# Sums of a graph layer turned in blocks on VectorE, attributes moved by five bits, and rows stored in rounds

## The chip, the core and the metric

The kernel runs on one core of one Trainium2 chip. The metric is the device time of one execution in microseconds, the median of the runs shown. The engines are called as in the profile: PE (TensorE), DVE (VectorE), ACT (ScalarE), POOL (GpSimd) and SP (SyncE, which here only issues DMAs).

## The reference

A message passing layer with a residual and a layer norm, over 50,000 nodes of 160 numbers (64 scalars `s`, 32 vectors `v` of 3) and 1,650,000 edges sorted by their destination. 800,000 of the edges are random, 800,000 are the same ones turned round, and 50,000 are loops from a node to itself.

```python
ss, vv = s[src], v[src]
e0, e1 = sh[:, 0:1], sh[:, 1:4]                  # 4 attributes per edge
dot = einsum('eui,ei->eu', vv, e1)
out0 = C0 * (ss * e0 @ W1 + dot * INV3 @ W2)
p3 = (ss @ W3)[:, :, None] * e1[:, None, :] * INV3
p4 = einsum('eui,uw->ewi', vv * e0[:, :, None], W4) * INV3
p5 = einsum('eui,uw->ewi', cross(vv, e1[:, None, :]), W5) * INV6
out1 = C1 * (p3 + p4 + p5)
m_agg = segment_sum(concatenate([out0, out1]), dst)
h = (m_agg scalars @ Ws, m_agg vectors @ Wv), scaled
x = layernorm(x + x + relu(h))
```

A message is linear in the row of the source and linear in the 4 attributes. So the kernel first sums, for each node and each attribute k, attribute k times the row of the source (4 x 160 numbers per node), and applies the weights to the sums: one matrix of 160 x 160 per attribute, in which W1 to W5 are already multiplied by Ws and Wv.

## The kernel before

**The units of work.** A unit is 128 edges. A group is 6 units, whose destinations fit into 32 consecutive nodes (W = 32 slots). Two groups make a pair (12 units), four groups a chunk (128 slots), and 20 groups, or 10 pairs, share one load of edges (table s). There are 1044 pairs, 522 chunks and 391 blocks of 128 output nodes. One long unrolled loop runs over the pairs.

**One pair.** POOL gathers the rows of the sources by 12 indirect DMAs, one per unit, into a tile `xg` (L304); there are four such tiles (`rows`, bufs=4). DVE makes `hot` (which of the 32 slots an edge falls into, L313) and `ha` (`hot` times each of the 4 attributes, L316), with three buffers. PE multiplies (L326): for each unit `ha` (128 edges x 4 x 32) against the gathered rows (128 edges x 160), summed over 6 units into `ps`, which holds 4 x 32 rows (attribute and slot) of 160 for each of two groups and has two buffers. ACT copies `ps` to `A` (L329).

**One chunk.** `turn` brings the feature axis to the partitions: PE transposes the four `A` in two parts, features 0 to 127 and 128 to 159 (`pt`, L564), and ACT copies each part to `at` (L567). `apply_weights` makes 8 products on PE (4 attributes x 2 parts of the features, `phc`, L578) and ACT copies the result to `hp` (L582).

**One block.** The loops from a node to itself are not gathered: `ahead` loads the block's own rows `xt` and their attributes `sa` (L593, L597), `own` transposes `xt` on PE (`ptx`, L616, two parts, with an ACT copy each, L617), multiplies by the weights (`yx`, L622, L623) and sums them with `sa` on DVE (`t`, L627, L629). `nodes` makes `hot2` (L606), which maps the slots of the chunks that may hold nodes of this block to its 128 nodes, and `block` sums the chunks' `hp` by it on PE (`phb`, L639, one product per chunk). How many chunks a block takes follows from bounds on where a chunk's nodes can lie (`off`, `low`, `high`, L200 to L206). Then follow relu, the residual and the norm on DVE (L175 to L190, with a root on ACT, L184), and SP sends `o` out (L737).

**The packs.** The loops must be taken out of the list of edges, and their attributes collected. The first 100 groups take the edges as they are; for the others 17 packs of 120 rows of 790 edges are worked on, beside the pairs, on DVE. A pack is a list of steps, spread over the pairs until it is due (`todo`, L796): read; `count`, `mark`, `examine`, `where` (find the loops and number them); `collect` (L471: for each of 31 places and 4 attributes one multiply with a sum over a stretch of the row, into `mine`); `shift` (L503 to L510: the remaining edges, `prow`, move left by 1, 2, 4, 8 and 16 places as the bits of their distance `far` say); then SP stores the rows to `edges` and `mine` to `selves` in DRAM at places held in registers (L543), first the even rounds of 10 rows, then the odd ones, then the heads of the rows again. Later loads of edges (L240) and `ahead` read these tables.

**What sets the order.** SP's order is the one in which the program is written (a manual schedule for SP, L766). PE, DVE, ACT and POOL run in the order that a scheduler finds; each engine then runs its list strictly in that order. `psM`, two buffers, is shared by `pt`, `phc`, `ptx`, `yx` and `phb`.

In the pair loop the change and the prediction touch these lines:

```python
rows = gather(placed[s], (g - s * SG) * G, ng * G, ...)     # L774
...
has[p + 1] = spread(placed[s1], (g1 - s1 * SG) * G, ng1 * G) # L778
sums.append(group_sums(p, rows, has.pop(p)))                 # L779
...
after_pair(p + 1, do_turn, c, sums)                          # L805
...
after_pair(p + 2, do_weights, c)                             # L811
```

## Time and profile before

| what | before |
|---|---|
| median of 3 runs (lowest, highest) | 20348.03 us (20332.03 to 20362.42) |
| the profiled execution | 20370.95 us |
| its span, first to last instruction | 20369.2 us |
| mean granted clock of PE | 0.663 |
| busy: POOL, PE, DVE, ACT | 11850.9, 10539.8, 6385.3, 1564.6 us |
| matmuls on PE | 47031 |
| gathers on POOL | 12522 |

A row of a group gives line, engine, operation, tiles and shapes, the count, then the busy time with the mean in ns of one, then the idle time of the engine just ahead of them and what ended it. A product in fp32 stands as two matmuls in these counts (25044 for 12522), a transpose as one. A row of waits gives the engine and what it did next, what it waited for, the time in all, how often, and the longest. "issue" is time in which the engine waited for nothing that the profile shows, "remote" is a release by something that it doesn't name. Times of a matmul's end are modelled.

### The profile page before, as it was taken

How to read it: one execution, taken by the hardware profiler on the slowest of the kernel's cores; microseconds unless marked ns; L12 is line 12 of the kernel's file. 1: busy time of each engine (PE TensorE's matmuls, PEld its weight loads, DVE VectorE, ACT ScalarE, POOL GpSimd, SP SyncE). 2: the span in 40 equal slices, each digit the busy share in tenths (PEclk: the TensorE clock that was granted, in tenths of full speed). 3: DMA queues.
4: the chain of work that ended last, by engine and by line, in shares of the span. 5: the costliest groups of instructions: out<-in, count | busy, mean ns of one | idle time of the engine just before them, and what ended most of it. 6: DMA issues, size and time to landing. Idle time of an engine off the chain costs nothing. (4 is left out here: it accounts for less than half of the span.)

```text
span 20369.2 us, 146272 instructions
## 1 busy us (share of the span) xinstructions
PE 10539.8 (52%) x47031; PEld 8362.9 (41%) x47032; DVE 6385.3 (31%) x15106; ACT 1564.6 (8%) x3876; POOL 11850.9 (58%) x12536
## 2 busy tenths in 40 slices
PE   5455545455454545555454545545454554545455
PEld 3343434334343434444443434434343443434444
DVE  3342423323242323323142333324232232413222
ACT  0000000000000000000000000000000000000000
POOL 6455655555565655555565655556565555656565
PEclk6666666666666666666666666666666666666666
DMA  2222222222222222222222222222222222222222
GB/s 63 58 55 62 58 63 58 59 60 61 60 59 63 58 59 61 61 60 57 65 57 64 58 60 61 60 57 61 63 57 59 61 61 58 60 61 59 58 61 55
DMA packets 809692, 1217.63 MB, mean 60 GB/s; under 512 B 283401, under 2 KB 587942, under 8 KB 804932
## 3 DMA queue, kind: packets, MB, share of 16 engines
q0 software_dynamic: 601056, 1026.60, 19.5%
q1 hardware_dynamic: 207256, 181.09, 3.3%
q8 instruction: 374, 6.13, 0.1%
q14 instruction: 398, 3.26, 0.1%
q10 hardware_dynamic: 608, 0.55, 0.0%
HBM read 1135.20 MB, written 72.13 MB: 59 GB/s over the span
## 5 line engine op out<-in xcount | busy, mean ns | idle before, releaser
L304 POOL DMA_INDIRECT xg<-in_x,si x12522 | 11846.6, 946 | 8441.8 <-issue 3609.6
L326 PE MATMUL ps<-xg,ha 128*128 128x160 f32 x25044 | 4929.5, 354 | 1846.3 <-issue 1601.1
L326 PEld LDWEIGHTS ps<-xg,ha 128*128 128x128 f32 x25044 | 4459.7, 233 | 2263.0 <-issue 1972.5
L316 DVE TENSOR_TENSOR ha<-hot,pk 128x1536 f32<-128x1536 f32 x1044 | 1820.5, 1747 | 3301.8 <-remote 2346.1
L616 PE MATMUL ptx<-ident,xt 128*128 128x128 f32 (+2 forms) x782 | 263.5, 337 | 3389.7 <-ACT xT L617 2563.9
L640 DVE TENSOR_TENSOR phb<-phb,t 128x160 f32<-128x160 f32 x391 | 129.8, 332 | 5466.4 <-remote 2231.4
L564 PE MATMUL pt<-ident,A 128*128 128x128 f32 (+1 forms) x4174 | 908.9, 361 | 1577.3 <-ACT hp L582 507.9
L616 PEld LDWEIGHTS ptx<-ident,xt 128*128 128x128 f32 (+2 forms) x782 | 100.4, 128 | 3545.3 <-ACT xT L617 2653.7
L471 DVE SCALAR_TENSOR_TENSOR pra<-marks,prow 120x236 bf16<-120x236 f32 (+40 forms) x2924 | 1491.9, 510 | 26.1 <-DVE pra L471 5.5
L578 PE MATMUL phc<-BWa,at 128*128 128x160 f32 x4176 | 940.7, 371 | 916.5 <-issue 741.4
L639 PE MATMUL phb<-hp,hot 128*128 128x160 f32 x4694 | 1057.9, 386 | 570.0 <-issue 487.4
L564 PEld LDWEIGHTS pt<-ident,A 128*128 128x128 f32 (+1 forms) x4174 | 557.5, 153 | 1901.9 <-issue 678.6
L578 PEld LDWEIGHTS phc<-BWa,at 128*128 128x128 f32 x4176 | 802.1, 243 | 1024.6 <-issue 834.3
L639 PEld LDWEIGHTS phb<-hp,hot 128*128 128x128 f32 x4694 | 951.4, 259 | 638.5 <-issue 533.1
L627 DVE TENSOR_SCALAR t<-yx,sa 128x160 f32<-128x160 f32 x391 | 149.6, 383 | 3274.9 <-PE yx L623 2287.1
L578 PE MATMUL phc<-BWb,at 32*128 32x160 f32 x4176 | 948.3, 374 | 397.3 <-issue 307.0
L623 PE MATMUL yx<-BWb,xT 32*128 32x320 f32 x1564 | 974.7, 718 | 182.4 <-issue 139.7
L578 PEld LDWEIGHTS phc<-BWb,at 32*128 32x128 f32 x4176 | 773.9, 236 | 545.8 <-issue 449.9
L567 ACT COPY at<-pt 128x512 f32<-128x512 f32 (+1 forms) x1044 | 600.5, 580 | 4909.6 <-remote 2561.2
L622 PE MATMUL yx<-BWa,xT 128*128 128x320 f32 x1564 | 923.2, 688 | 5.5 <-issue 3.1
L329 ACT COPY A<-ps 128x320 f32<-128x320 f32 x1044 | 440.0, 422 | 4581.1 <-remote 2777.5
L629 DVE SCALAR_TENSOR_TENSOR t<-yx,sa,t 128x160 f32<-128x160 f32 x1173 | 448.0, 382 | 847.1 <-remote 454.1
(147 smaller groups left out, 4931.8 us busy)
## 6 DMA issues: line engine op xcount, KB each, us to landing
xg<-in_x,si POOLq DMA_INDIRECT x12522
edges<-prow SPq DMA_DIRECT2D x1994, 18.5 KB
r<-edges SPq DMA_DIRECT2D x99, 360.0 KB
selves<-mine SPq DMA_DIRECT2D x1992, 0.5 KB
xt<-in_x SPq DMA_DIRECT2D x390, 80.0 KB
out<-o SPq DMA_DIRECT2D x390, 80.0 KB
pra<-in_attr SPq DMA_DIRECT2D x16, 1481.2 KB
edges<-prow SPq DMA_DIRECT2D x997, 0.8 KB
```

The source lines that it names most:

```text
L304: nc.gpsimd.indirect_dma_start(out=xg[:, j, :], out_offset=None, in_=x, in_offset=bass.IndirectOffsetOnAxis(ap=placed[0][:, u + j:u + j + ...
L316: nc.vector.tensor_tensor(ha[:, :n], hot[:, :n].unsqueeze(2).to_broadcast([P, n, NK, W]), pk[:, :, u:u + n].rearrange("p k u -> p u k").un ...
L326: nc.tensor.matmul(ps[:, j // G, :], ha[:, j].rearrange("p k w -> p (k w)"), xr, start=j % G == 0, stop=j % G == G - 1)
L329: evict(A[:, :ng], ps[:, :ng])
L471: nc.vector.scalar_tensor_tensor(T["waste"][:n, w0:w1], T["marks"][:n, w0 - a:w1 - a], float(w + 1), T["rows"][:n, w0:w1, 2 + k], op0=ALU. ...
L564: nc.tensor.transpose(pt[:f1 - f0, g, :], A[:, i, f0:f1], ident)
L567: evict(at[:, :, :ng].rearrange("f k g w -> f g k w"), pt[:f1 - f0, :ng].rearrange("f g (k w) -> f g k w", w=W))
L578: nc.tensor.matmul(ph[:ng * W], at[:, k, :ng].rearrange("f g w -> f (g w)"), bw[:, k, :], start=i == 0, stop=i == 2 * NK - 1)
L622: nc.tensor.matmul(y[:nb], xT[:, 0, :nb], BWa[:, ks, :], start=True, stop=False)
L623: nc.tensor.matmul(y[:nb], xT[:D - P, 1, :nb], BWb[:, ks, :], start=False, stop=True)
L629: nc.vector.scalar_tensor_tensor(t[:nb], y[:nb, i], sa[:nb, k:k + 1], t[:nb], op0=ALU.mult, op1=ALU.add)
L639: nc.tensor.matmul(ph[:nb], hot2[:r, i, :nb], hp[:r], start=i == 0, stop=i == len(cs) - 1)
```

## The change

**Sums.** `group_sums` no longer copies `ps` to `A`. DVE transposes `ps` in blocks of 32 x 32 straight into `sums`, a tile [128, 5, 4, 32] per chunk: partition k * 32 + f holds feature 32 b + f of attribute k, for block b of the features, group and slot. `turn` is gone with its transposes on PE and its copies on ACT. The weights are laid out to match (`BWk`: the same 128 rows, 5 blocks), and `apply_weights` makes 5 products over 128 rows in place of 8. `BWk` and `BWh` are built through a table in DRAM at the start.

**The block's own rows.** `own` transposes two parts of 80 features, copies both at once on ACT, and multiplies by `BWh`, the weights in two parts of 80; the number of products stays.

**The packs.** 16 packs of 128 rows in place of 17 of 120. `where` and `collect` go. `aim` takes for each loop the distance from its place in the row to its number, as five bits plus a mark of 32 (L468 and on of the new file); the attributes `pra` move left by these bits as the rows do, in a pass of their own ahead of that for `prow`; `pick` clears what has no mark, and one reduction over the row sums the places w, w + 32, w + 64 and so on into `mine`. The rows are stored in 16 successive rounds of 8, and the heads of one round only. Two more empty steps stand ahead of the stores.

**Bounds and checks.** The bounds on a chunk's nodes are set for each tenth of the edges by themselves, so that a block takes 4 or 5 chunks (before 5 or 6): 1737 products `phb` in place of 2347. The checks on these bounds run some 9 pairs ahead of the end and not behind the last pair.

```diff
+    cuts = sorted({0, NH // QG, NCH} | {round(i * NCH / 10) for i in range(10)})
...
+        off = 5 * math.sqrt(n_edges * max(0, t * (1 - t))) / (degree - 1) + 10
+        bounds += [(-off, 0.75 * step + W + off)] * (c1 - c0)
...
-        def group_sums(p, rows, ha):
+        def group_sums(p, rows, ha, at, i):
...
-            A = sump.tile([P, PG, D], F32, name="A")
-            evict(A[:, :ng], ps[:, :ng])
-            return A, ng
+            nc.vector.transpose(at[:, :, i:i + ng, :].rearrange("p b g w -> p g b w"),
+                                ps[:, :ng].rearrange("p g (b f) -> p g b f", f=FB))
...
+            def aim(h, a, e):
+                m, to = T["marks"][:n], T["hit"].bitcast(I32)[:n, a:e]
+                q = slice(0, e - a)
+                nc.vector.tensor_tensor(to, place_[:n, a:e], m[:, q], op=ALU.subtract)
+                nc.vector.tensor_scalar(to, to, W - 1, W, op0=ALU.bitwise_and, op1=ALU.bitwise_or)
+                nc.vector.scalar_tensor_tensor(to, m[:, q], 0.0, to, op0=ALU.is_gt, op1=ALU.mult)
...
+            def pick(a, e):
+                m = T["marks"][:n, 0:e - a]
+                nc.vector.tensor_scalar(m, T["hit"].bitcast(I32)[:n, a:e], float(W), None, op0=ALU.is_equal)
+                pra = T["pra"][:n, a:e]
+                nc.vector.tensor_tensor(pra, pra, m.unsqueeze(2).to_broadcast([n, e - a, NK]), op=ALU.mult)
+
+            def collect():
+                nc.vector.tensor_reduce(T["mine"][:n], T["pra"][:n].rearrange("p (m w) k -> p w k m", w=W),
+                                        axis=AX.X, op=ALU.add)
...
+            for far, what, all_ in (("hit", "pra", True), ("far", "prow", False)):
+                g = moves(far, what, all_)
+                steps += [partial(next, g, None)] * (4 * KM.bit_length() - (0 if all_ else 2))
+                if all_:
+                    steps += [partial(pick, a, e_) for a, e_ in halves] + [collect]
+            steps += [None, None]
             steps += [None, None]
...
-            for head, j0 in ((False, 0), (False, 1), (True, 0)):
-                for j in range(j0, RS, 2):
-                    steps += [partial(store, head, j), None, None, None]
+            for head, j in [(False, j) for j in range(RS)] + [(True, 0)]:
+                steps += [partial(store, head, j), None, None, None]
...
-        def turn(pairs):
...
+            for b in range(ND):
+                nc.tensor.matmul(ph[:ng * W], at[:, b, :ng].rearrange("p g w -> p (g w)"), BWk[:, b, :], start=b == 0, stop=b == ND - 1)
```

How the order moves is shown at two places. The first is PE near pair 444, in the middle of the program, before the change: `ps` are the products of pairs, `pt` the turn of `A`, `phc` the weights, `ptx` and `yx` the block's own rows. The number behind a name tells one buffer's use from another.

```order
L578 MATMUL phc_38944<-BWa_69,at0_38886 128x160 x4
L578 MATMUL phc_38944<-BWb_70,at128_38893 128x160 x4
L326 MATMUL ps_39224<-xg_39207,ha_39100 128x160 x12
L326 MATMUL ps_39314<-xg_39297,ha_39222 128x160 x12
L616 MATMUL ptx_39052<-ident_60,xt_38622 128x128
L616 MATMUL ptx_39052<-ident_60,xt_38622 32x128
L622 MATMUL yx_39059<-BWa_69,xT_39053 128x320
L623 MATMUL yx_39059<-BWb_70,xT_39053 128x320
L622 MATMUL yx_39064<-BWa_69,xT_39053 128x320
L623 MATMUL yx_39064<-BWb_70,xT_39053 128x320
L564 MATMUL pt_39071<-ident_60,A_38795 128x128 x2
L564 MATMUL pt_39071<-ident_60,A_38925 128x128 x2
```

After the change, PE at pair 444 (`sums` takes the place of `at`):

```order
L572 MATMUL phc_31020<-BWk_70,sums_30833 128x160 x5
L608 MATMUL ptx_31066<-ident_60,xt_30869 80x128 x2
L340 MATMUL ps_30989<-xg_30972,ha_30946 128x160 x12
L616 MATMUL yx_31072<-BWh_69,xT_31069 128x320 x2
L340 MATMUL ps_31050<-xg_31032,ha_30987 128x160 x12
L616 MATMUL yx_31077<-BWh_69,xT_31069 128x320 x2
L340 MATMUL ps_31126<-xg_31109,ha_31047 128x160 x8
L284 MATMUL bank_120<-first_31088,ones_124 128x20
```

And DVE there, after the change, where `ha_31047` is the operand of the pair behind `ps_31050`:

```order
L326 TENSOR_TENSOR hot_31045<-bank_120,rel_30512 128x384
L342 STREAM_TRANSPOSE sums_31049<-ps_31050 128x2x5x32
L329 TENSOR_TENSOR ha_31047<-hot_31045,pk_30505 128x1536
L497 TENSOR_SCALAR marks_29647<-pri_29577 128x395
L620 TENSOR_SCALAR t_31071<-yx_31072,sa_30871 128x160
L504 COPY_PREDICATED prow_29643<-marks_29647,prow_29643 128x2274
L622 SCALAR_TENSOR_TENSOR t_31071<-yx_31072,sa_30871,t_31071 128x160
L283 TENSOR_SCALAR first_31088<-starts_126,r6_30814 120x20
```

The four transposes `pt` per part have gone from PE, and of the weights' eight products five are left. On DVE the transposition of `ps_31050` stands ahead of `ha_31047`, so that the next products, `ps_31126`, come behind both. Counted over the program, the next pair's `ha` stands behind the transposition in 257 of 1044 pairs, the one after it in 341, and later ones in the rest. The last row but two, L504, is also the last shift of a pack, of `prow_29643`.

The second place is the first store of a pack. SP before the change, a pack in the middle of the program (`prow_34572` is its tile):

```order
L737 DMA out_0<-o_36131 128x160
L593 DMA xt_36326<-in_x 128x160
L597 DMA sa_36328<-selves_123 128x4
L737 DMA out_0<-o_36272 128x160
L593 DMA xt_36490<-in_x 128x160
L597 DMA sa_36492<-selves_123 128x4
L526 TENSOR_LOAD spots_161
L543 DMA edges_122<-prow_34572 1x18960
```

And DVE before, at the last shift of the same pack (`r6_36771` is the next load of edges, which SP issues 21 rows behind the store above):

```order
L510 COPY_PREDICATED prow_34572<-marks_34576,prow_34572 120x2322
L503 TENSOR_SCALAR marks_34576<-pri_34513 120x411
L510 COPY_PREDICATED prow_34572<-marks_34576,prow_34572 120x2370
L503 TENSOR_SCALAR marks_34576<-pri_34513 120x395
L510 COPY_PREDICATED prow_34572<-marks_34576,prow_34572 120x2274
L190 TENSOR_SCALAR o_37311<-y_37106,mv_37110,rstd_37241 128x160
L270 TENSOR_SCALAR first_37243<-starts_126,r6_36771 120x20
```

SP after the change, at the store of the pack `prow_29643` whose last shift on DVE was shown above:

```order
L728 DMA out_0<-o_30792 128x160
L585 DMA xt_30968<-in_x 128x160
L589 DMA sa_30970<-selves_123 128x4
L728 DMA out_0<-o_30917 128x160
L585 DMA xt_31082<-in_x 128x160
L589 DMA sa_31084<-selves_123 128x4
L539 TENSOR_LOAD spots_161
L556 DMA edges_122<-prow_29643 1x18960
```

Before, SP has sent 151 results `o` when it comes to this store, while DVE has made 154 when it comes to the shift that the store needs. After, it is 138 on both. In the packs behind the third, SP came to the store 2 or 3 results ahead of DVE's last shift before, and comes to it at the same count now.

More of the change, by code (lines that the diff above doesn't have):

```diff
@@ L63 @@
 QG = P // W
+FB = P // NK
+ND = D // FB
 PG = 2
@@ L438, in mark @@
             def mark(h, a, e):
-                rows, m, cum, far = T["rows"], T["marks"][:n], T["cum"], T["far"]
+                rows, m, cum, far = T["prow"], T["marks"][:n], T["cum"], T["far"]
                 q = slice(0, e - a)
@@ L702, in tile_gnn_resnorm @@
         place_ = once.tile([P, L], F32, name="place")
+        chunk_ = once.tile([P, NCH], F32, name="chunk")
         later = {}
```

253 lines of the change are left out of this document (110 added, 143 removed).

## The prediction

> **What bounds the kernel now.** I read the page's busy times first, then the groups of instructions by line, the waits, the stretches of PE around POOL's pauses, and the timeline at two places. The first rows of the page are the span and the busy time of each engine.
>
> ```profile
> span 20369.2 us, 146272 instructions
> ## 1 busy us (share of the span) xinstructions
> PE 10539.8 (52%) x47031; PEld 8362.9 (41%) x47032; DVE 6385.3 (31%) x15106; ACT 1564.6 (8%) x3876; POOL 11850.9 (58%) x12536
> ```
>
> No engine is full, so the end is set by order and waits. The busiest is POOL, and nearly all of it is one group, the gathers; its waits are listed next (line, what it waited for, us in total, times, longest).
>
> ```profile
> L304 POOL DMA_INDIRECT xg<-in_x,si x12522 | 11846.6, 946 | 8441.8 <-issue 3609.6 <-PE ps L326 3483.5 <-remote 1119.0
> ```
> ```profile
> POOL xg L304 <- issue: 3609.6, 11821, 1.6
> POOL xg L304 <- PE ps L326: 3483.5, 291, 97.1
> POOL xg L304 <- remote: 1119.0, 327, 6.6
> ```
>
> A gather holds POOL for 0.946 us and its issue costs 3609.6/11821 = 0.305 us. That makes 1.251 us, 15.0 us for the 12 of a pair, and 12522 x 1.251 = 15,666 us: POOL's floor. The other 4,600 us are waits, 3483.5 + 1119.0 = 4602.5, in 618 pauses. The long ones (291, mean 12.0 us) end with PE's products L326, which free a buffer of gathered rows; the 327 called remote have a mean of 3.4 us. So POOL runs until its four buffers are full and then waits for PE: PE's chain bounds the kernel, though PE looks half idle.
>
> Why it is slow shows in stretches of PE cut at POOL's starts and stops in the last part, where no pack runs: for each of four runs of POOL the first 10 us, the other 20 us (two pairs), and the pause behind it. The columns are start:end, length, PE busy with its matmuls, the granted clock, the DMA share and GB/s.
>
> ```profile
> 19433.40:19443.40 10.00, 9.99 (x54) 0.72 0.23 59
> 19443.40:19463.40 20.00, 6.80 (x32) 0.64 0.25 66
> 19463.40:19468.00 4.60, 2.81 (x7) 0.50 0.07 18
> 19468.00:19478.00 10.00, 9.81 (x43) 0.75 0.29 74
> 19478.00:19498.00 20.00, 5.40 (x25) 0.63 0.25 66
> 19498.00:19504.80 6.80, 6.80 (x26) 0.50 0.06 14
> 19522.30:19532.30 10.00, 7.56 (x35) 0.73 0.47 108
> 19532.30:19552.30 20.00, 10.74 (x27) 0.55 0.26 68
> 19552.30:19560.00 7.70, 2.94 (x12) 0.50 0.04 11
> 19560.00:19570.00 10.00, 10.00 (x68) 0.91 0.23 57
> 19570.00:19590.00 20.00, 6.82 (x27) 0.64 0.25 66
> 19590.00:19594.30 4.30, 1.36 (x5) 0.50 0.07 19
> ```
>
> Behind a pause PE starts (54+43+35+68)/4 = 50 matmuls in 10 us; in the next 20 us of the same run only (32+25+27+27)/4 = 27.8, so 1.4 per us against 5. A pause of 23.4/4 = 5.85 us adds 50/4 = 12.5. That is 90 matmuls in two pairs, and the kernel has 47031/1044 = 45.0 per pair: the cycle closes. PE can start only so many matmuls per cycle, and POOL pauses until they are done. How a late stretch looks is seen in the timeline (start, length, work; idle before):
>
> ```profile
> 19523.82 5.39 PE L326 MATMUL ps<-xg,ha 128*128 128x160 f32 x24
> ...
> 19535.27 0.42 ACT L329 COPY A<-ps 128x320 f32<-128x320 f32 x1 [8.81 <-remote]
> ```
>
> The products end at 19529.2, ACT reads them at 19535.3: 6.1 us late, with ACT idle. While POOL has gathered for some time, what PE finished reaches others late, and each handover from PE costs about this.
>
> **The change on PE.** The rows of PE that the change touches (busy us, mean ns):
>
> ```profile
> L639 PE MATMUL phb<-hp,hot 128*128 128x160 f32 x4694 | 1057.9, 386 | 570.0 <-issue 487.4 <-ACT at L567 81.7
> ...
> L578 PE MATMUL phc<-BWb,at 32*128 32x160 f32 x4176 | 948.3, 374 | 397.3 <-issue 307.0 <-ACT at L567 85.8 <-ACT prow L410 1.5
> L578 PE MATMUL phc<-BWa,at 128*128 128x160 f32 x4176 | 940.7, 371 | 916.5 <-issue 741.4 <-ACT at L567 172.3 <-DMA BWa<-BVd 1.9
> ...
> L564 PE MATMUL pt<-ident,A 128*128 128x128 f32 (+1 forms) x4174 | 908.9, 361 | 1577.3 <-ACT hp L582 507.9 <-DVE t L629 378.9 <-issue 343.2
> ```
>
> A product is two matmuls in these counts, a transpose one. The turn's transposes go: -4174. Eight products of the weights become five: 8352 x 3/8 = -3132. The tighter bounds take 1737 instead of 2347 products for the blocks: -610 x 2 = -1220. Together -8526 of 47031, 18%: 36.9 per pair instead of 45.0. By the means above that is 4174 x 0.361 + 3132 x 0.372 + 1220 x 0.386 = 3.1 ms of PE's 10.5 ms. Two handovers between PE and ACT per chunk (ps to A, pt to at) become one from PE to DVE. The products of the pairs, of which POOL's buffers wait, stay.
>
> Now the sum, against the profiled execution: 20370.95 us, span 20369.2, which is 0.1% over the median of the three times. By the stretches, two pairs need 73.8 matmuls, and a run of 30 us starts 77.8. So a pause has no backlog left to wait for; it stays only because without it PE would fall to the 1.4 per us of a late stretch, 21 in a pair, against 36.9. So I let all 618 pauses be of the short kind: 618 x 3.4 = 2,115 us. What the long ones hold above that is 3483.5 - 291 x 3.4 = 2,490; 420 of it goes to the stores (below), and of the 2,070 left I keep a quarter, 520, for places where PE's rows come in a bunch. Waits 2,635 instead of 4,602: 20369 - 1967 = 18,400 us. The other way, a cycle of two pairs with one pause of the shortest shown with its run, 4.3 us, gives 522 x 4.3 = 2,245 us of waits and 18,000. If single pairs each need a 3.4 us pause, it is 1044 x 3.4 = 3,550 and 19,300.
>
> **The stores and the loads behind them.** SP's first store of each pack waits until DVE has done the last shift, and the next load of packed edges stands behind it on SP; PE's transposes of that load hold all of PE behind them.
>
> ```profile
> SPq L543 <- DVE prow L510: 4021.9, 17, 300.5
> ```
> ```profile
> PE pk L287 <- DMA r<-edges: 669.0, 15, 49.0
> ```
> ```profile
> 9621.59 0.49 PE L287 MATMUL pk<-ident,r 120*128 120x120 f32 x1 [40.89 <-DMA r<-edges]
> ...
> 9638.12 0.94 POOL L304 DMA_INDIRECT xg<-in_x,si  x1 [31.17 <-PE ps L326]
> ```
>
> SP waits 4021.9/17 = 237 us per pack, PE 669.0/15 = 44.6. At the place shown PE's 40.9 us cost POOL 31.2. So 15 x 44.6 x 31.17/40.89 = 510 us, less 15 ordinary pauses of 5.85, 88: 420 us. In the new order SP reaches the store just where DVE comes to the last shift (the rows of both, with the change), so this goes. If it does not, the forecast is 18,820. The stores themselves (fewer in the head, eight instead of ten per round) lie on SP, which has that slack.
>
> **The change on DVE.** Rows of DVE and one of ACT:
>
> ```profile
> L471 DVE SCALAR_TENSOR_TENSOR pra<-marks,prow 120x236 bf16<-120x236 f32 (+40 forms) x2924 | 1491.9, 510 | 26.1 <-DVE pra L471 5.5 <-remote 4.5 <-DVE hot L313 4.0
> ...
> L313 DVE TENSOR_TENSOR hot<-bank,rel 128x384 f32<-128x384 f32 x1044 | 559.4, 546 | 1.4
> ...
> L510 DVE COPY_PREDICATED prow<-marks,prow 120x2370 f32<-120x2370 int32 (+7 forms) x170 | 471.4, 2773 | 1.2
> ...
> L329 ACT COPY A<-ps 128x320 f32<-128x320 f32 x1044 | 440.0, 422 | 4581.1 <-remote 2777.5 <-PE ps L326 1311.7 <-PE phb L639 159.8
> ```
>
> The collecting goes: at least -1,492. The five-bit shift of the attributes is 10 steps per pack: a predicated copy of 1580 numbers, by L510's 2773 ns for 2370 about 1.85 us, and four small operations of 395 columns, by L313's 546 ns for 384 about 0.56 each: 41 us, x 16 packs = 656. Aim, pick and the one reduction are some 14 us per pack by the same rates, 220. The turns are new: 1044 transposes of 128x320 out of PSUM, which no row shows; ACT's copy of the same tile, 422 ns, is the lower bound (440 us), three times that the upper one (1,320). I take DVE's own read of PSUM of about that size, L313's 546: 570 us. DVE's sum is -1492 + 656 + 220 + 570 = -46: it stays near 6.3 ms (7.1 at the upper bound), a third of the span, and costs nothing as busy time: it is hidden beside POOL. ACT loses its copies and stays far from any bound.
>
> The Trainium skill, in VectorE: DVE Perf Modes, section The three transpose paths, gives 311 ns for a 128x128 bf16 transpose on VectorE, in 32x32 blocks only; as an estimate that is 778 ns for 320 columns and 0.81 ms in all. No row here shows it, and by it too DVE would stay at a third of the span.
>
> The exchange, eviction on DVE instead of ACT, adds a wait on an engine that runs in order: behind a transposition that waits for PE stand the operands ha of the next pairs and all pack steps. The checks moved ahead of the end can save no more than what of the span is neither gathers nor those pauses, 20369 - 15666 - 4602 = 101 us; the weights at the start are a few DMAs more. I count both together as nothing.
>
> **The rivals.**
> *DVE's order (slower).* In 257 of 1044 pairs the next pair's ha stands behind the transposition, so PE cannot begin it before DVE has seen the late end of the last. The example's lateness is 6.1 us, and ha and the transposition follow. PE has other rows there in nearly all. The gain of 1,970 us is used up when each costs 1970/257 = 7.7 us, and at 10 us the time is 20369 - 1967 + 2570 = 20,970. For it: the lateness is of that size. Against: POOL's four buffers are 60 us of cover, and only in 105 of the 257 places does the order hold fewer than 12 other matmuls between the two pairs. Chance 0.08.
>
> *PE's load is not what sets the pauses.* If the pauses follow from the lateness alone, however few rows PE has, only the stores' part goes: 20369 - 420 = 19,950. For it: PE busy 52%. Against: the cycle closes with the number of matmuls. Chance 0.15.
>
> *The pauses vanish.* If PE keeps up without pauses, POOL's floor is left, 15,666 + 101 = 15,770, up to 16,600 with a quarter of the short pauses. For it: 77.8 starts against 73.8 needed. Against: 1.4 per us in late stretches. Chance 0.05.
>
> *The clock (slower).* The granted clock is 0.50 in every pause, (0.72+0.75+0.73+0.91)/4 = 0.78 in the 10 us behind it and 0.62 after. If with less work PE stays at 0.50 throughout, a run starts 50 x 0.50/0.78 + 27.8 x 0.50/0.62 = 54.5 matmuls; 19.3 of the 73.8 are left for the pause, at 12.5/5.85 = 2.1 per us 9.0 us, 522 x 9.0 = 4,700 us of waits and 20,470. It decides once the bursts fall below 0.55 or so. Against: the bursts come at full speed right behind pauses at 0.50. Chance 0.03. The Trainium skill has such a rule, in TensorE: Matmul & The Clock Gate, Part 1: after an idle window of some 3.4 us the clock of PE is halved until it has been busy as long. The rows agree as far as 0.50 in each pause goes.
>
> *It does not do what it says* (the gain of one part is lost in another): within 41 us of before. Chance 0.04.
>
> **How the numbers follow.** The likeliest case is 18,400 with 0.65, its own range 17,200 to 19,400. Faster by over 0.2% (41 us, about what a measurement of this kernel can tell from none) come the forecast, 0.65, the second rival, 0.15, and the vanished pauses, 0.05: 0.85. The same: 0.04. Slower: 0.08 + 0.03 = 0.11. The range takes in the forecast and the second rival, 17,200 to 19,960 (its low end is a mean pause of 1.4 us for each pair, between the floor and the forecast); left out are the vanished pauses, no change and the slower cases, 0.20.
>
> **What would show it.** Right: PE has about 38,500 matmuls; POOL's waits fall to about 2,600 us with the count near 600; PE's wait for loaded edges (669.0) is gone; DVE is busy 6.0 to 6.6 ms. Wrong: POOL's waits stay above 4,000 us with PE's count down (second rival), or DVE's ha shows long waits for its own transposition's products and PE waits long for ha (the first). A POOL busy without long pauses would be the third.

## The result, and the profile after

The changed kernel takes 19558.55 us (median of 4 runs, 19533.00 to 19572.49) against 20355.22 us (4 runs) of the kernel before: a ratio of 0.9606 (95% interval 0.9590 to 0.9623), 797 us less. Forecast were 18,400 us and 1,967 us less. The sign and the range held, and less than half of the gain came.

The page of the changed kernel, its first rows.

```profile
span 19555.8 us, 118643 instructions
## 1 busy us (share of the span) xinstructions
PE 8526.2 (44%) x38505; PEld 7238.9 (37%) x38506; DVE 6029.3 (31%) x11070; ACT 504.2 (3%) x1392; POOL 11855.8 (61%) x12536
```

PE has the 38,505 matmuls that were forecast and is 2.0 ms less busy, where 3.1 ms were forecast; DVE is a little less busy, not more. POOL's waits, in the same columns as before:

```profile
POOL xg L317 <- issue: 3660.3, 12000, 1.8
POOL xg L317 <- PE ps L340: 2934.4, 254, 43.1
POOL xg L317 <- remote: 942.8, 223, 9.6
```

The two kinds of pause were 3483.5 and 1119.0 us, 4,602 in all. They are 2934.4 + 942.8 = 3,877 now. The difference of 725 us is most of the gain, and the time is still POOL's floor plus its pauses. The number of pauses fell from 618 to 477, but their mean did not fall to the short kind's 3.4 us: it went from 7.4 to 8.1 us.

Where the long ones are comes out when the idle time of POOL is summed by the place of a pair in its table of edges (10 pairs share one). I summed what each gather waited beyond the usual 0.305 us of issue, for all 1044 pairs; the number in brackets is how many pairs waited over 2 us.

```
kernel                               all      first pair of a table    the other nine
before                              4,623      1,405 (75)              3,218
changed                             3,843      1,853 (96)              1,990
changed, PE in the written order    2,392         54 (13)              2,338
before, PE in the written order     3,134        119 (44)              3,015
before, packs and bounds alone      4,099        954 (84)              3,145
```

(The last three rows are experiments, below.) In the changed kernel nearly half of POOL's waiting stands at one pair in ten, 1,853/96 = 19 us each. One such place in the timeline of the changed kernel, around the table that begins at pair 610:

```profile
11429.85 3.01 PE L572 MATMUL phc<-BWk,sums 128*128 128x160 f32 x10 [0.84 <-DVE t L622]
...
11436.71 0.65 PE L608 MATMUL ptx<-ident,xt 128*80 128x128 f32 x2 [3.85 <-DVE phb L633]
...
11452.77 0.52 DVE L342 STREAM_TRANSPOSE sums<-ps 128x320 f32<-128x320 f32 x1 [15.54 <-remote]
...
11454.25 0.37 ACT L610 COPY xT<-ptx 80x256 f32<-80x256 f32 x1 [1.19 <-remote]
11454.67 4.63 PE L616 MATMUL yx<-BWh,xT 80*128 80x320 f32 x8 [17.31 <-ACT xT L610]
...
11465.25 0.27 PE L300 MATMUL pk<-ident,r 120*128 120x120 f32 x1
...
11476.94 5.32 PE L340 MATMUL ps<-xg,ha 128*128 128x160 f32 x38
...
11477.92 0.94 POOL L317 DMA_INDIRECT xg<-in_x,si  x1 [27.92 <-PE ps L340]
```

PE's transposes `ptx` end at 11437.4; ACT reads them at 11454.3, 16.9 us late. PE runs its list in order, and behind `yx`, which needs that copy, stand the sums and weights of several chunks, the transposes of the next table (`pk`), and only then the products for which POOL's buffers wait. POOL has stopped at 11450.0 and starts at 11477.9. Most of PE's 17.31 us of waiting lie ahead of that pause; in the pause PE works off what has piled up. The stretches of PE there (in the columns of the prediction) say the same:

```profile
11414.50:11424.50 10.00, 9.42 (x53) 0.83 0.25 68
11424.50:11450.00 25.50, 6.66 (x27) 0.59 0.29 72
11450.00:11478.20 28.20, 21.65 (x106) 0.76 0.28 92
11478.20:11488.20 10.00, 10.00 (x75) 1.00 0.34 102
11488.20:11508.20 20.00, 8.34 (x31) 0.65 0.27 66
```

53 starts in 10 us, then 27 in 25 us: the pattern of before. But the pause holds 106 matmuls, where the prediction's sum left a pause no backlog.

### The profile page after: what moved, and what is told of

Its sections match the earlier page's. It is cut to its first block, busy times and chain, and to the rows that moved or that the text cites. A ratio compares the mean times of both kernels' runs of the same rounds, so it can differ in the third digit from the quotient of the medians.

```text
span 19555.8 us, 118643 instructions
## 1 busy us (share of the span) xinstructions
PE 8526.2 (44%) x38505; PEld 7238.9 (37%) x38506; DVE 6029.3 (31%) x11070; ACT 504.2 (3%) x1392; POOL 11855.8 (61%) x12536
## 4 chain that ended last, share of the span: by engine, by line
another core or an unknown queue 43%; PE 18%; issue 18%; POOL 11%; DVE 8%; DMA 1%; ACT 1%; DVEq 0%; SPq 0%; ACTq 0%; POOLq 0%
POOL xg L317 11%; PE ps L340 10%; PE yx L616 4%; PE phc L572 2%; PE phb L632 2%; DVE ha L329 2%; DMA xg<-in_x,si 1%; DVE t L622 1%; DVE prow L504 1%; DVE hot L326 0%; DVE sums L342 0%; PE ptx L608 0%; DVE pra L504 0%; ACT xT L610 0%
## 5 line engine op out<-in xcount | busy, mean ns | idle before, releaser
L342 DVE STREAM_TRANSPOSE sums<-ps 128x320 f32<-128x320 f32 x1044 | 530.6, 511 | 7579.5 <-remote 4673.7
L616 PE MATMUL yx<-BWh,xT 80*128 80x320 f32 x3128 | 1449.7, 621 | 3135.8 <-ACT xT L610 1941.1
L616 PEld LDWEIGHTS yx<-BWh,xT 80*128 80x128 f32 x3128 | 786.8, 266 | 3577.7 <-ACT xT L610 2074.4
L572 PE MATMUL phc<-BWk,sums 128*128 128x160 f32 x5220 | 1106.5, 361 | 703.9 <-issue 356.8
L572 PEld LDWEIGHTS phc<-BWk,sums 128*128 128x128 f32 x5220 | 980.9, 239 | 794.5 <-issue 458.2
L632 PE MATMUL phb<-hp,hot 128*128 128x160 f32 x3474 | 768.0, 373 | 655.0 <-issue 250.4
L326 DVE TENSOR_TENSOR hot<-bank,rel 128x384 f32<-128x384 f32 x1044 | 551.9, 541 | 0.1
L504 DVE COPY_PREDICATED prow<-marks,prow 128x2370 f32<-128x2370 int32 (+8 forms) x160 | 444.4, 2778 | 0.0
L504 DVE COPY_PREDICATED pra<-marks,pra 128x1580 f32<-128x1580 int32 (+8 forms) x160 | 305.8, 1911 | 0.0
L598 DVE TENSOR_TENSOR hot<-bank,rr 128x512 f32<-128x512 f32 (+2 forms) x391 | 285.3, 730 | 0.0
```

Source lines behind the costliest of these rows:

```text
L326: nc.vector.tensor_tensor(hot[:, :n], slotsP[:, 0:W].unsqueeze(1).to_broadcast([P, n, W]), rel[:, u:u + n].unsqueeze(2).to_broadcast([P, n ...
L342: nc.vector.transpose(at[:, :, i:i + ng, :].rearrange("p b g w -> p g b w"), ps[:, :ng].rearrange("p g (b f) -> p g b f", f=FB))
L504: nc.vector.copy_predicated(what[:n, a:e], mi[:, r].unsqueeze(2).to_broadcast([n, e - a, what.shape[2]]), what[:n, a + d:e + d])
L572: nc.tensor.matmul(ph[:ng * W], at[:, b, :ng].rearrange("p g w -> p (g w)"), BWk[:, b, :], start=b == 0, stop=b == ND - 1)
L598: nc.vector.tensor_tensor(hot2[:, :len(cs)], slotsP.unsqueeze(1).to_broadcast([P, len(cs), P]), rr[:, :len(cs)].unsqueeze(2).to_broadcast( ...
L616: nc.tensor.matmul(y[:nb], xT[:, i, :nb], BWh[:, i, ks, :], start=i == 0, stop=i == 1)
```

## The experiments

Two theories were to be told apart. The **load**: the number of PE's matmuls sets the pauses, as predicted, 189 us for one matmul per pair. The **order**: bunches in PE's scheduled order set them, many matmuls of blocks, weights and tables in one piece, behind which the products wait. Counted in the traces, the changed kernel has 56 bunches of 60 or more matmuls between two products, the longest of 118 (the expectations below say 114), the kernel before 31, the longest of 106. Each of the 56 stands ahead of the products of the seventh pair of a table and holds the transposes for the next table. With four tiles of gathered rows, POOL feels it four pairs on, at the next table's first pair.

The runs came to two kinds of chips. On some the kernel before takes 20,350 to 20,380 us as in the result; there PE's results are seen late. On the others it takes 15,827 to 15,864. All runs, each against the kernel before on its own chip:

| run | PE's results late | us | kernel before there | ratio (95%) |
|---|---|---|---|---|
| changed kernel (the result) | yes | 19558.55 | 20355.22 | 0.9606 (0.9590 to 0.9623) |
| pe_in_order_4 | yes | 18150.92 | 20370.40 | 0.8913 (0.8888 to 0.8939) |
| all_but_sums_2 | yes | 19821.54 | 20370.40 | 0.9734 (0.9706 to 0.9762) |
| before_pe_in_order_2 | yes | 18899.73 | 20358.96 | 0.9283 (0.9239 to 0.9328) |
| five_row_buffers_2 | yes | 19093.28 | 20358.96 | 0.9378 (0.9351 to 0.9405) |
| half_gathers_before | yes | 12238.29 | 20377.25 | 0.6005 (0.5974 to 0.6036) |
| half_gathers_changed | yes | 11184.01 | 20377.25 | 0.5488 (0.5459 to 0.5517) |
| half_gathers_pe_in_order | yes | 9805.73 | 20377.25 | 0.4811 (0.4797 to 0.4826) |
| changed_again | no | 15746.33 | 15862.18 | 0.9919 (0.9895 to 0.9942) |
| pe_in_order | no | 15705.29 | 15827.33 | 0.9922 (0.9906 to 0.9939) |
| pe_in_order_2 | no | 15746.14 | 15862.18 | 0.9925 (0.9903 to 0.9948) |
| pe_in_order_3 | no | 15706.43 | 15828.41 | 0.9923 (0.9894 to 0.9952) |
| all_but_sums | no | 15710.17 | 15827.33 | 0.9925 (0.9909 to 0.9942) |
| sums_alone | no | 15823.00 | 15827.33 | 0.9997 (0.9987 to 1.0007) |
| bounds_alone | no | 15818.06 | 15827.33 | 0.9994 (0.9984 to 1.0003) |
| before_pe_in_order | no | 15817.14 | 15864.22 | 0.9970 (0.9951 to 0.9990) |
| five_row_buffers | no | 15744.49 | 15864.22 | 0.9925 (0.9896 to 0.9953) |
| half_gathers_sums_alone | no | 8984.24 | 15828.41 | 0.5676 (0.5660 to 0.5693) |
| half_gathers_all_but_sums | no | 8093.23 | 15828.41 | 0.5113 (0.5098 to 0.5128) |

### The parts one by one, where nothing is late

Four kernels went together to a chip of the second kind: the changed kernel with PE in the written order, and the kernel before with one or two parts of the change.

```diff
 # pe_in_order, on the changed kernel
-        later_pools.enter_context(tc.manual_schedule(engines={ET.SP}))
+        later_pools.enter_context(tc.manual_schedule(engines={ET.SP, ET.PE}))
 # sums_alone, on the kernel before: group_sums, apply_weights, own and the weights of the change
+            nc.vector.transpose(at[:, :, i:i + ng, :].rearrange("p b g w -> p g b w"),
+                                ps[:, :ng].rearrange("p g (b f) -> p g b f", f=FB))
 # bounds_alone, on the kernel before: cuts and bounds of the change
+        bounds += [(-off, 0.75 * step + W + off)] * (c1 - c0)
 # all_but_sums: bounds_alone, with RP, RS, aim, shift, pick, collect and the stores of the change
+            for head, j in [(False, j) for j in range(RS)] + [(True, 0)]:
```

The line of pe_in_order sets PE's order alone, but the scheduler then finds other orders for DVE and ACT too: in the traces the next pair's `ha` stands behind the transposition in 172 pairs, where it was 257. What is called the written order below is the whole of this; PE's share in it was not run apart.

> The changed kernel, with PE's instructions in the order in which the program is written (as SP's already are) instead of the scheduler's; nothing else differs, the number of matmuls stays 38,505. Of the 3,838 us that POOL waits in the changed kernel, 1,852 stand at the first pair of a table of edges (96 pauses), behind bunches of up to 114 matmuls in PE's order; in the written order no bunch is over 20. Theory of the load (the number of matmuls sets the pauses, as predicted): no change, 19,560 us within 1%. Theory of the order (what was gained in matmuls is lost again to the bunches): the waits at the first pairs fall to the mean of the other pairs, 1,986/940 = 2.1 us, or 220 in all, so 19,560 - 1,630 = 17,930 us; half of that if other waits grow.

> The kernel before, with only the sums turned on DVE, the 5 products of the weights per chunk and the block's own rows in two parts of 80. 7,306 matmuls fewer (7.0 per pair). Theory of the load: by the prediction's term, 1,547 us for 8.2 matmuls per pair, 189 us each, so 20,350 - 1,320 = 19,030 us. Theory of the order: under 400 us of gain, and bunches at the first pair of each table as in the changed kernel. Rival of DVE's order: slower than before.

> The kernel before, with only the tighter bounds (1,737 products for the blocks in place of 2,347, 1,220 matmuls fewer, 1.2 per pair). Theory of the load: 1.2 x 189 = 220 us of gain, 20,130 us. Theory of the order: under 100 us, 20,250 to 20,400 us, by chance of where the scheduler puts things.

> The kernel before, with the tighter bounds and the new packs (attributes moved by five bits, 16 packs, stores in successive rounds) but the old turn of the sums on PE and ACT. Prediction: the wait of PE for loaded edges goes (420 us) and the bounds give 220: 19,710 us. Theory of the order: the 420 us come, the rest does not: 19,930 us. If the wait stays, SP's order was not its cause: above 20,100 us.

Measured were 15705.29, 15823.00, 15818.06 and 15710.17 us, where the kernel before took 15827.33. Both theories missed, because there POOL hardly waits. The waits of POOL in bounds_alone:

```profile
POOL xg L308 <- issue: 3584.1, 11765, 0.6
POOL xg L308 <- PE ps L330: 254.6, 587, 58.0
```

Most of the 587 are the issue of 0.3 us with another name: beyond that POOL waits 120 us in the whole run. And a result of PE is read as soon as it is there:

```profile
10011.02 0.90 PE L330 MATMUL ps<-xg,ha 128*128 128x160 f32 x2 [0.32 <-DMA xg<-in_x,si]
...
10012.02 0.43 ACT L333 COPY A<-ps 128x320 f32<-128x320 f32 x1 [11.24 <-PE ps L330]
```

The product ends at 10011.92 and ACT reads it at 10012.02, 0.10 us later, with POOL in full run; the prediction's example has 6.1 us. So POOL's floor of 15,666 us bounds both kernels there. What is left of the change is the packs' part: all_but_sums gives 117 us, the sums 4 and the bounds 9, both within what can be told from nothing. In all_but_sums POOL's waits beyond the issue are 9 us, against 120 in bounds_alone, whose long ones end with products of PE (58.0 at most).

### Is it the chip?

> The changed kernel itself. The first four runs came to another base than the result: the kernel before took 15,827 us there, against 20,355, with POOL pausing 3 times in place of 620, so on such a chip POOL's 12,522 gathers are the bound. Theory: the time depends on how late PE's results reach the others while POOL gathers, and that differs from chip to chip. If the chip shows no lateness: the changed kernel is at POOL's floor, 15,700 us, 0.8% under the kernel before. If it does: 19,560 us against 20,355, as in the result. Rival: the four runs were shorter by what they changed: then the changed kernel is at 19,560 us here while the kernel before is at 15,827.

> The changed kernel with PE in the written order. If the kernel before is at 15,830 us on this chip: 15,705 us again, POOL's floor, and nothing is told apart. If it is at 20,350 us: theory of the load 19,560 us within 1%, theory of the order 17,930 us, with the waits at the first pair of a table fallen from 1,852 to some 220 us.

It is. The unchanged files took 15746.33 and 15862.18 us there. On such a chip the written order is worth nothing more, 15705 to 15746 us in three runs.

### Half the gathers

To see what POOL's gathering does to PE, every second gather was left out (the sums are then of other rows).

```diff
-            for j in range(n - len(others)):
+            for j in range(0, n - len(others), 2):
...
-            return [xg[:, j, :] for j in range(n - len(others))] + others
+            return [xg[:, j - j % 2, :] for j in range(n - len(others))] + others
```

> The kernel before with every second gather left out (a unit's product takes the rows gathered for the unit ahead of it, so the sums are of other rows; all else stays). POOL's floor falls to 6,261 x 1.251 = 7,830 us and PE becomes the bound. On a chip without lateness: PE's busy time of some 12,100 us with the waits of its order, 12,300 to 14,000 us. On a chip with lateness, theory that lateness comes from POOL's gathering: well under 17,000 us, the released PE shows it; rival, that PE's results are late there whatever POOL does: above 18,000 us.

> The changed kernel with every second gather left out, as above. Theory of the load (the time follows PE's matmuls where PE bounds): 38,505/47,031 = 0.82 of the kernel above. Theory of the order: PE's order holds back what the fewer matmuls give, 0.92 to 1.0 of it. Rival of DVE's order (PE waits behind transpositions): over 1.0.

> The changed kernel with every second gather left out and PE in the written order. Theory of the load: the same time as with the scheduler's order, within 3%. Theory of the order: at least 5% shorter, since no bunch of more than 20 matmuls stands ahead of the products.

These three came to a chip where results are late: 12238.29, 11184.01 and 9805.73 us, far under 17,000. So the lateness hangs on POOL's gathering. The changed kernel is at 0.914 of the kernel before, where the load alone gave 0.82 and the order at least 0.92; the written order takes another 12.3% off. POOL's waits in the changed kernel, and then with PE in the written order:

```profile
POOL xg L317 <- PE ps L340: 2686.4, 304, 37.6
```
```profile
POOL xg L317 <- issue: 1686.6, 5507, 1.8
POOL xg L317 <- PE ps L340: 1281.1, 348, 13.1
```

At the first pairs of tables POOL waits 1,722 us in the changed kernel and 68 in the written order. The load can't say that, since the matmuls are the same.

Two parts with half the gathers, and once more the written order with all of them:

> The changed kernel with PE in the written order, all gathers kept. Of the chips so far two show no lateness (the kernel before at 15,830 to 15,860 us), two do (20,350). With half the gathers the written order took 12% off on a chip with lateness and the waits of 25 us were gone. If this chip shows lateness: theory of the order 17,930 us (the waits at the first pairs of tables, 1,852 us, fall to 220), theory of the load 19,560. If it shows none: 15,705 to 15,746 us as before, POOL's floor.

> The kernel before with every second gather left out, and only the sums turned on DVE with the 5 products and the two parts of 80. With half the gathers the kernel before took 12,238 us and the changed one 11,184, 1,054 us less, on a chip with lateness. Theory of the load: the sums take 7,306 of the 8,526 matmuls that go, so 0.86 of the part of the gain that is not the loads' wait: 11,640 us (1,054 - 350 for the loads, x 0.86 = 600). Theory of the order: it is the sums' part that bunches PE's order, 12,000 us or more. On a chip without lateness: 0.85 of the same kernel's time with all matmuls.

> The kernel before with every second gather left out, the tighter bounds and the new packs, but the old turn on PE and ACT. Theory of the load: 350 us for the loads' wait and 100 for the bounds, 11,790 us where the kernel before takes 12,238. Theory of the order: the larger part of the 1,054 us, below 11,600.

They met a chip without lateness: 15706.43, 8984.24 and 8093.23 us. The kernel before with half the gathers was not run there, so their gain is not known, but they can be compared with each other: the kernel with 45,811 matmuls, the old turn and the new packs is 891 us faster than the one with 39,725, the new turn and the old packs. With sums_alone's edit POOL waits 1,110 us, 821 of it at first pairs of tables; with all_but_sums' 208, 56 of it there. PE waits for the operands that stand behind the transpositions on DVE, 718.0 us with the new turn and 110.4 with the old. The row of the kernel with the new turn:

```profile
PE ps L334 <- DVE ha L323: 718.0, 223, 18.0
```

So PE waits for DVE's operands with no lateness at all, and longer with the new turn. Whether the turn costs more than its matmuls save isn't shown: the slower kernel also keeps the old packs, with 287.3 us in which PE waits for loaded edges and three pauses of POOL of 49 to 75 us in its first 850 us.

### The order and the parts, where results are late

> The changed kernel with PE in the written order, all gathers kept. On a chip with lateness (the kernel before at 20,350 us): theory of the order 17,930 us, the waits at the first pairs of tables fallen from 1,852 to about 220 us (with half the gathers they fell from 1,722 to 68); theory of the load 19,560. On a chip without: 15,705 us.

> The kernel before with the tighter bounds and the new packs, but the old turn of the sums on PE and ACT. On a chip with lateness: theory of the load as predicted, 420 us for the loads' wait and 220 for the bounds, 19,710 us, and the sums would give 150 more of the 797; theory of the order (the sums' saving in matmuls is lost to the bunches it makes): the same time as the changed kernel or less, 19,200 to 19,600 us. On a chip without: 15,710 us.

18150.92 and 19821.54 us, against 20370.40. The written order takes 1,408 us off the changed kernel; 1,630 were expected of it. The waits at first pairs fell from 1,853 to 54 us, as expected, while those of the other pairs rose from 1,990 to 2,338. POOL's rows:

```profile
POOL xg L317 <- issue: 3643.3, 11912, 1.8
POOL xg L317 <- remote: 1322.4, 315, 7.9
POOL xg L317 <- PE ps L340: 933.4, 207, 11.9
```

No pause is over 11.9 us, against 43.1. The packs and the bounds together give 549 us (640 were predicted), near the load's 19,710 us and outside the 19,200 to 19,600 of the theory of the order. That leaves 797 - 549 = 248 us for the sums, with 7.0 of the 8.2 matmuls per pair: by the load's term 1,320. The table of places (with the result) shows where the rest went. From packs and bounds alone to the whole change the other nine pairs lose 1,155 us of POOL's waits, but the first pairs gain 899. The bunches of 60 or more go from 24 to 56 there. How much of the 1,155 is fewer matmuls, and how much is work that moved from the nine pairs into the bunch, these runs don't separate.

### The kernel before in that order, and a buffer more

```diff
 # five_row_buffers, on the changed kernel
-            tc.tile_pool(name="idx", bufs=2) as idxp, tc.tile_pool(name="rows", bufs=4) as rowp, \
+            tc.tile_pool(name="idx", bufs=2) as idxp, tc.tile_pool(name="rows", bufs=5) as rowp, \
```

> The kernel before with PE in the written order. Against the changed kernel in the written order (18,151 us on a chip with lateness) it tells what 18% fewer matmuls and the new packs are worth where no bunch holds them back. Theory of the load, by the prediction's sum of 1,967 us: 20,120 us, with the loads' wait of 420 in it. Theory of the order alone (the number of matmuls matters little): 420 us above the changed kernel in that order, 18,570 us. On a chip without lateness: 15,830 us, since the loads' waits stay.

> The changed kernel with five tiles of gathered rows in place of four, 15 us more of cover for POOL. Theory of the order: the 1,852 us at the first pairs of tables, 96 pauses of 19 us, shrink by up to 15 us each, and the time by up to 1,440 us: 18,200 to 18,700 us on a chip with lateness. Theory of the load: a buffer more only moves the pauses, 19,560 us within 1%. On a chip without lateness: 15,705 us.

These came to a chip without lateness, 15817.14 and 15744.49 us, and told nothing of the question. Repeated where results are late:

> The kernel before with PE in the written order. On a chip with lateness: theory of the load, by the prediction's sum, 20,120 us; theory of the order alone, 18,570 us, 420 above the changed kernel in that order. On a chip without lateness: 15,780 to 15,820 us again.

> The changed kernel with five tiles of gathered rows. On a chip with lateness: theory of the order 18,200 to 18,700 us, the pauses at the first pairs of tables each up to 15 us shorter; theory of the load 19,560 us within 1%. On a chip without: 15,705 to 15,745 us again.

The kernel before with PE in the written order takes 18899.73 us, between the two values. POOL's waits in it:

```profile
POOL xg L304 <- issue: 3597.5, 11720, 2.3
POOL xg L304 <- PE ps L326: 1530.3, 198, 79.9
POOL xg L304 <- remote: 1438.7, 474, 8.2
```

So the order is worth 20,359 - 18,900 = 1,459 us in the kernel before and 1,408 in the changed one, and the change is worth 749 us in the written order (18,900 - 18,151) and 797 in the scheduled one. The ratio of change to before is 0.8913/0.9283 = 0.960 in the written order and 0.9606 in the scheduled one. The change is worth about the same in both orders, though not by the same parts: the loads' wait is not among PE's waits in the kernel before in the written order, so the 749 us hold none of it, while in the scheduled order its end is part of what the packs give.

Five tiles give 465 us. Both theories missed: the order let 860 to 1,360 be expected, the load no more than 1%. The waits at first pairs fell only from 1,853 to 1,314, and a wait for `si` appears that the kernel with four tiles doesn't have:

```profile
POOL xg L317 <- PE ps L340: 1166.3, 211, 16.8
POOL xg L317 <- DVE si L302: 1095.8, 76, 31.9
```

With a buffer free, POOL comes to the next table and its indices `si` are not there: PE's transposes for them stand behind the same bunch.

### What a pause consists of

With the bunches gone, the pauses show a pattern. For each run of POOL between two pauses of over 1 us, counted in pairs, the median of the pause behind it (us), with the number of such runs:

```
kernel                              after 1 pair    2 pairs       3 pairs      4 pairs
before                              2.51 (261)      6.47 (319)    5.99 (39)
changed                             2.48 (76)       4.33 (266)    6.00 (77)    7.95 (48)
before, PE in the written order     2.34 (422)      4.61 (281)    8.67 (18)
changed, PE in the written order    2.43 (142)      4.48 (357)    6.43 (59)
half gathers, changed, written      1.47 (384)      2.41 (287)    3.89 (25)
```

In the written order a pause costs about 2.2 us per pair that POOL gathered ahead of it, some 0.2 us for each gather, whether PE has 45 or 37 matmuls per pair, and 0.5 to 0.6 of that where a pair has half the gathers. That would be 1044 x 2.2 = 2,300 us in each kernel with all its gathers where results are late. The 2.2 us are read off these runs, and no run tests them by themselves. What POOL waits above 2.2 us per pair (summed over the pauses more than 1 us above it) is 2,282 us before, 1,678 in the changed kernel, 780 before in the written order, and 84 in the changed kernel in the written order. By this the last one has little left to lose: 15,666 + 2,300 + 101 = 18,070 us, and it takes 18,151.

## Why the prediction was wrong

**Held.** The number of matmuls (38,505), the sign, and the range of 17,200 to 19,960 us; the likeliest case's own range, 17,200 to 19,400, was missed. The loads' wait is gone, as SP's new place among the instructions said: the transposes of loaded edges wait 3.7 us in all, where they waited 669.0.

```profile
L300 PE MATMUL pk<-ident,r 120*128 120x120 f32 (+1 forms) x400 | 92.2, 316 | 3.7 <-issue 3.7
```

By all_but_sums_2 the packs and bounds give 549 us, and the waits at first pairs fall by 1,405 - 954 = 451; 420 were forecast for the loads, which were not run alone.

**Failed, but not in the sum: PE's busy time.** It fell by 2.0 ms and not 3.1. The working multiplied counts by the mean time of one matmul, but matmuls overlap: the products L326 have 25,044 x 354 ns = 8.9 ms by their mean and 4929.5 us of busy time. By busy time the rows of the prediction give 908.9 + 3/8 x (948.3 + 940.7) + 1220/4694 x 1057.9 = 1.9 ms.

**Held roughly.** DVE's own time: forecast -46 us, measured 6029.3 - 6385.3 = -356. The rows of the transposition and of the attributes' shift, as they came out:

```profile
L342 DVE STREAM_TRANSPOSE sums<-ps 128x320 f32<-128x320 f32 x1044 | 530.6, 511 | 7579.5 <-remote 4673.7 <-PE ps L340 2322.6 <-issue 301.1
...
L504 DVE COPY_PREDICATED pra<-marks,pra 128x1580 f32<-128x1580 int32 (+8 forms) x160 | 305.8, 1911 | 0.0
```

511 ns against the 546 taken, and 1911 against 1,850. What was left out of the sum as "at least", the accumulator reads of the collecting (235.9 us) and `where` (76), is about the difference. The estimate that the prediction made from the Trainium skill, VectorE: DVE Perf Modes, The three transpose paths, 778 ns, is too high by half here: the measurement decides.

**Failed: the size of the load's term.** The step was "So I let all 618 pauses be of the short kind", with "what the long ones hold above that" put down to PE's backlog, and "a quarter, 520, for places where PE's rows come in a bunch". With it the load was worth 1,547 us, and POOL's waits were to fall by 1,967. They fell by 725, and the whole change gave 797 us, of which 549 come with packs and bounds. The waits above 3.4 us per pause are 3,877 - 477 x 3.4 = 2,255 us, where the sum kept 520. Three things were wrong in it.

First, the long pauses were not backlog that follows from the number of matmuls. Before, 1,405 us of the waits stood at the first pairs of tables; the prediction took 420 of that as the loads' wait and the rest as load. The kernel before in the written order shows 119 us there with every matmul still in place. A bunch costs no less with 37 matmuls per pair than with 45. Those of 60 matmuls or more take 55.0 us in the mean before and 57.5 after, from one product to the next, and PE is busy in 23.5 and 23.4 of that: more than half is waiting (17.31 us for one late handover in the example). POOL's longest pause at each has a mean of 24 us before and 27 after. On a chip without lateness (changed_again) the same 56 bunches take 26.4 us with PE busy in 21.1, and POOL doesn't pause at them: it takes the bunch and the lateness together. And the scheduled order of the changed kernel has more of them, 56 for 31. PE's order as it stands ahead of the prediction, near pair 444, is at none of these places. The prediction kept 520 us for bunches, and 1,853 us stand at first pairs.

Second, where the order is even the number of matmuls counts, but for less: 749 us for 8.2 matmuls per pair, 91 us each and not 189, if all of it is put down to them (the fewer handovers and the new packs were not taken apart there). Above its pauses of 2.2 us per pair the kernel before in that order has 780 us to give, and the change takes 700 of them.

Third, the short pauses were taken as fixed in number (618 x 3.4 us). By the table of pauses they follow the pairs gathered, 2.2 us for each, whether they come one by one or in twos. The cycle of two pairs with one pause of 4.3 us, from which the other way of the sum got 18,000 us, is what the changed kernel does in the written order (357 runs of two pairs, median pause 4.48 us, 18,151 us). The scheduled order breaks that cycle once in ten pairs.

**The rivals.** "PE's load is not what sets the pauses" (19,950 us) is partly borne out: by the table of pauses some 2,300 us of the pauses follow POOL's gathers, and the waits of 3,877 us stand just under its sign of 4,000. It is not all, as the written order shows. DVE's order makes PE wait longer for `ha`, before and in the changed kernel:

```profile
PE ps L326 <- DVE ha L316: 105.8, 37, 12.6
```
```profile
PE ps L340 <- DVE ha L329: 633.2, 146, 23.4
```

That is 527 us more of PE's waits, against the 1,970 us of time that would have used up the gain; what the 527 cost in time isn't shown. The clock's rival fell: the mean granted clock is 0.656 after 0.663, and bursts reach 1.00 (what the prediction called full speed is 0.72 to 0.91 in its rows). In the Trainium skill, TensorE: Matmul & The Clock Gate, Part 1, idle windows bring the clock down. The rows of the prediction have 0.50 in each pause, and the long pause shown here, with PE busy in 21.65 of 28.20 us, has 0.76; the changed kernel with less work on PE was not slower in either kind of chip.

**The best version.** The changed kernel with PE in the written order: 0.8913 of the kernel before where results are late (0.8888 to 0.8939), and 0.992 of it, like the changed kernel, where they are not.

## What to carry to other kernels

Before a saving is priced from an engine's rate, sort the waits that it is to remove by their place in the loop: 1,405 us that stand at one pair in ten are not load but something that happens there. And read the new order of the engine that others wait for: a bunch of a hundred instructions ahead of what releases a buffer cost POOL as much after the work was cut by a fifth as before. One line that keeps that engine in the written order was worth 1,400 us where results are late, nearly twice the whole change, and nothing more where they are not.

## What the runs showed of the hardware

The same kernel takes 20,350 to 20,380 us on some chips and 15,827 to 15,864 on others, 29% apart, with the same 946 ns per gather and the same 0.30 us of issue. On the first kind what PE has finished is often seen late (6.1 us, 16.9 us) once POOL has issued indirect gathers for some time, and in time again when POOL pauses. Counted over the handovers of PE to an idle ACT or DVE in the kernel before, the share that comes over 1 us late is 8% in POOL's pauses of over 2 us, 7% in the first 5 us behind one, 49% from 5 to 15 us and 77% later. Of some 3,600 such handovers in bounds_alone, on the other kind, none is over 1 us late. On the first kind POOL stopped for about 0.2 us per gather in the written order. With half the gathers the kernel before took 12,238 us on such a chip. What in the chip makes the difference stays open: no run here tells it.
